# Cross-attention and quantised FFN on one core: two bias rows moved from TensorE to GpSimd, and a rewritten last half with filler matmuls on TensorE

## Chip, core and metric

The kernel runs on one NeuronCore of a Trainium2 chip. The metric is the device time of one execution in microseconds (us), lower is better. Engines are called as in the profile: PE (TensorE matmul), PEld (its weight loads), DVE (VectorE), ACT (ScalarE), POOL (GpSimd), SP (SyncE, which only issues DMAs here).

## What is computed

The reference, cut to what matters (4 batches of 1024 rows, width 256, 16 heads of 16, context of 77 rows, hidden width 1024):

```python
x = x + xattn(layernorm(x), ctx)          # Wout product + bout
x = x + ffn(layernorm(x))                 # w_proj product + b_proj

def xattn(x, mem):                        # keys: 77 context rows, then x itself
    q = x @ Wq;  k, v = split(concat(mem, x) @ Wkv)
    dots = q k^T * 16**-0.5, causal over x, all context visible
    return softmax(dots) @ v @ Wout + bout

def ffn(x):                               # both products on quantised operands
    h = block_quant(x) @ block_quant(w_fc).T + b_fc
    return block_quant(gelu(h)) @ block_quant(w_proj).T + b_proj
```

`block_quant` works on blocks of 32 along the contracted dimension: the block's largest magnitude gives a power of two, and values are rounded to 3 mantissa bits of it. The kernel does this with three steps: a reduce (largest magnitude per block), two small operations that turn it into a constant "mag", then an add of mag and a subtract of mag, which rounds.

## The kernel before, in words

Rows are handled in tiles of 128 (8 per batch, T = 32 in all). Four heads form a group, so there are 16 stages `kk` (4 batches of 4 groups). In each stage, 14 steps go over pieces of the causal score matrix; a step is two half steps. In a half step PE does the row maxima of the next stage (L563, `max_matmul`, K = 32, four of them in the four 32-row strips of the array), the scores of this stage (L627, also K = 32), and attention times values with a lag of two steps (L664, which uses all 128 rows). DVE reduces the maxima (L587, L589), ACT takes the exponentials (L638), POOL sets masked entries to zero (L643) before L664 reads them.

Everything else is cut into units, each a list of emitted stages with delays, which `run` (L1357) places into the half steps by a planner's budget: a unit has a cost in us, each of its stages a load on DVE, PE, POOL, ACT, and a stage is emitted when its delay is over and the credit of its engines is positive. Emission order is queue order: every engine runs its instructions in the order in which they are emitted. The units that the change touches:

- `bias_units` (L113) loads the three bias vectors, splits them in three bf16 parts and builds `bias3` (3 x 1536). A bias is added on PE: a matmul of `ones3` (3 x 128) with a slice of `bias3` as the last member of an accumulation group (L813 for the attention output, L965 for the FFN output, L900 for the hidden layer).
- `wout_unit` (L797): fetches a tile of x (L804, on SP's queue), multiplies attention output with Wout (L809, two f32 products) and adds the bias (L813), copies the sum out of PSUM on ACT (`evacuate`, L794), adds it to x on POOL (L817), and takes statistics. Its fetch waits until the half is `divided`, that is until the attention sums have been normalised.
- `out_unit` (L921): quantises the hidden tile, transposes it (L954), multiplies with w_proj (L962, eight products), adds the bias (L965), evacuates (L794), adds on POOL (L969) and stores.
- `last_divide` (L747) normalises a half of the last batch: sums to DRAM and back (`sm`), a reciprocal, to DRAM and back (`rows`), then two PE products that spread the rows over partitions (L768) and two DVE multiplications (L776).

The last batch has no later stage to hide behind. Its first half's output tiles run as units in stage 15, directly on DVE. The rest is `last_part` (L1099): a list of jobs, each with an engine, an estimated time, predecessors and, for PE jobs, a PSUM bank (three `s` banks, two `st` pairs). A greedy loop takes the job that can start soonest by these estimates and emits it. The jobs of a tile are `norm` (ACT), `largest` (DVE), `round` (POOL), `turn` (PE transposes, L1168), `turned` (ACT), `hidden` (PE, L896 and L900), `gelu` (ACT, L1187), `max0`, `max1` (DVE, L197 and the small L204 and L208), `add0` (DVE, L224), `add1` (POOL, L224), `sub0`, `sub1` (POOL, L229), `turn_h` (PE, L1221), `turned_h` (ACT, L1229), `project` (PE, L1236 and L1240) and `finish` (DVE, L1247, then the store L1248). The second half's tiles first need `fetch`, `invert`, `spread`, `scale`, `load` (x, L1116), `wout` (L1124, L1128), `add`, `stats` and `root`.

A start-up row of 100 matmuls of the identity (`identb`, L1417) runs on PE while the first inputs load; its results are not used.

Of the kernel before, what the change touches and what calls it, by code (L numbers as in the profile page):

```python
# [9 lines left out]
F32 = mybir.dt.float32  # L10
# [33 lines left out]
def kernel(  # L44
# [68 lines left out]
    def bias_units(dram):  # L113
# [10 lines left out]

        def split():
            for r in range(3):
                nc.vector.tensor_copy(parts[r], braw)
                if r < 2:
                    nc.vector.tensor_sub(braw, braw, parts[r])
# [8 lines left out]

    wfcT = const.tile([P, KC, HID], BF16, name="wfcT")
# [117 lines left out]
    with ExitStack() as actx:  # L257
# [489 lines left out]
        def last_divide(b, ic):  # L747
# [17 lines left out]
            def spread(k):  # L765
                def emit():
                    got[k] = s_tile([P, ICW])
                    nc.tensor.matmul(  # L768
                        got[k], sel[:, k, :], got["rows"], start=True, stop=True
                    )  # L770
                return emit
# [24 lines left out]

        def wout_unit(b, it):  # L797
# [4 lines left out]
            def fetch():  # L802
                x2[t] = xrp.tile([P, D], F32, name="x2")
                nc.sync.dma_start(out=x2[t], in_=xf[t * P : (t + 1) * P, :])  # L804

            def project():
                yp = s_tile([P, D])
                for k in range(KC):
                    nc.tensor.matmul(  # L809
                        yp, o_pk[b, ic][:, k, it * P % ICW : it * P % ICW + P], wo_sb[:, k, :],  # L810
                        start=(k == 0), stop=False,
                    )
                nc.tensor.matmul(yp, ones3, bias3[:, B_OUT : B_OUT + D], start=False, stop=True)  # L813
# [10 lines left out]
            if b == B - 1:  # L824
# [4 lines left out]
                return cost(1.8, [fetch, project, (1, add_and_collect)])  # L829
            return cost(  # L830
                1.8, [fetch, project, (2, add), (2, collect)],
                (0, 0, 0, 0), (0, 0.4, 0, 1.1), (0, 0, 0.7, 0), (0.6, 0, 0, 0),
# [59 lines left out]
        def hidden_matmuls(t):  # L892
            hp = ps_st.tile([P, 2, ICW], F32, name="st_ps")
            for n in range(HID // ICW):
# [26 lines left out]
        def out_unit(t):  # L921
# [28 lines left out]

            def turn():
# [7 lines left out]
            def project():  # L959
                yp = s_tile([P, D])  # L960
                for k in range(HC):
                    nc.tensor.matmul(  # L962
                        yp, got["hT"][:, k, :], wprT[:, k, :], start=(k == 0), stop=False
                    )
                nc.tensor.matmul(yp, ones3, bias3[:, B_PROJ : B_PROJ + D], start=False, stop=True)  # L965
                got["y"] = evacuate(yp)

            def add():
# [7 lines left out]
                [first, (1, largest(1)), (1, rounding(0)), (1, rounding(1)), turn, project, (2, add)],  # L976
                (0.7, 0, 0, 0), (1.05, 0, 0, 0), (0, 0, 2.1, 0), (0, 0, 2.1, 0), (0, 1, 0, 0.6),
# [121 lines left out]
        def last_part(b):  # L1099
# [4 lines left out]
            fetch, invert, parts = last_divide(b, 1)  # L1104
            jobs, banks = {}, {"s": (3, []), "st": (2, [])}
            got = {}
# [6 lines left out]
            def load(t):  # L1113
                def emit():
                    x2[t] = xrp.tile([P, D], F32, name="x2")
                    nc.sync.dma_start(out=x2[t], in_=xf[t * P : (t + 1) * P, :])  # L1116
                return emit

            def project(t):
                def emit():  # L1120
                    col = t * P % ICW
                    got["yp", t] = s_tile([P, D])
                    for k in range(KC):
# [28 lines left out]
            def largest(t):  # L1152
                def emit():
                    got["magx", t] = quant_steps(got["xh", t], D, "x")
# [9 lines left out]
            def turn(t):  # L1164
                def emit():
                    got["tp", t] = s_tile([P, KC, P], BF16)
# [12 lines left out]
            def hidden(t):  # L1179
                def emit():  # L1180
                    got["hp", t] = hidden_matmuls(t)
                return emit

            def gelu(t):
                def emit():
                    hs[t] = hp_.tile([P, HID], F32, name="h")
                    nc.scalar.activation(  # L1187
                        hs[t], got["hp", t].rearrange("p e n -> p (e n)"), AF.Gelu
                    )
# [6 lines left out]
            def largest_h(t, p):  # L1196
                def emit():
                    if p == 0:
                        got["amax", t] = small.tile([P, HID // QBLK], F32, name="amaxh")
                    quant_largest(hs[t][:, cols[p]], got["amax", t][:, blocks[p]])  # L1200
                    if p:
                        got["magh", t] = quant_mag(got["amax", t], "h")
                return emit

            def add_h(t, p, engine):
                return lambda: quant_add(engine, hs[t][:, cols[p]], got["magh", t][:, blocks[p]])
# [10 lines left out]
            def turn_h(t):  # L1217
                def emit():
                    got["tp", t] = s_tile([P, HC, P], BF16)
# [12 lines left out]
            def project_h(t):  # L1232
                def emit():
                    got["yp", t] = s_tile([P, D])
                    for k in range(HC):
# [9 lines left out]
            def finish(t):  # L1245
                def emit():
                    nc.vector.tensor_tensor(x2[t], x2[t], got["yp", t], ALU.add)  # L1247
                    nc.sync.dma_start(out=of[t * P : (t + 1) * P, :], in_=x2[t])  # L1248
                return emit


            job("fetch", "SP", 0.5, fetch, late=3.5)
            job("invert", "DVE", 0.6, invert, ["fetch"], late=4.2)
            for k, (spread, scale_sums) in enumerate(parts):
                job(("spread", k), "PE", 1.2, spread, ["invert"], "s", ("scale", k))
                job(("scale", k), "DVE", 0.8, scale_sums, [("spread", k)])
            for i in range(HN, NT):
                t = T[i]
                job(("load", i), "SP", 0.5, load(t), late=2.0)
                job(  # L1260
                    ("wout", i), "PE", 1.8, project(t), [("scale", k) for k in range(KC)], "s",
# [9 lines left out]
            for i, t in enumerate(T):  # L1271
# [3 lines left out]
                job(("largest", i), "DVE", 0.9, largest(t), [("norm", i)])  # L1275
                job(("round", i), "POOL", 1.3, rounding(t), [("largest", i)] + old("turn", XQ))
                job(("turn", i), "PE", 0.4, turn(t), [("round", i)], "s", ("turned", i))
# [3 lines left out]
                job(("hidden", i), "PE", 2.0, hidden(t), [("turned", i)], "st", ("gelu", i))  # L1281
                job(("gelu", i), "ACT", 1.05, gelu(t), [("hidden", i)] + old("sub1", HBUF))
                job(("max0", i), "DVE", 0.7, largest_h(t, 0), [("gelu", i)])
                job(("max1", i), "DVE", 1.1, largest_h(t, 1), [("max0", i)])
# [240 lines left out]
```

## Time and profile before

| What | Value |
|---|---|
| runs shown | 1002.62, 1004.85 (median), 1007.97 us |
| profiled execution, its own time | 1001.35 us |
| its span in the profile | 999.6 us (1.75 us lie around it) |
| mean granted PE clock over the span | 0.971 |
| end of the last attention product of the last stage (L664) | about 929.1 us |
| end of the last PE work before `last_part` (L813) | 931.6 us |
| last instruction of `last_part` on DVE (L1247) | 996.43 to 996.85 us |
| matmuls of `bias3` with 256 columns: L813, L965, L1128, L1240 | 28, 24, 4, 8 |

The profile lists busy time per engine; for PE a matmul's end is modelled, and matmuls overlap, so the distance between the starts of two instructions says more than their durations. "PEclk" is the share of PE's clock that was granted in a slice or a stretch. In groups and timelines a row reads: line, engine, operation, output<-inputs, shape, count, then busy time and mean ns, or start and duration. In the view of stretches a row reads: stretch, its length, busy us and instruction counts of PE, PEld, DVE, ACT, POOL, then PEclk, DMA share and GB/s.

### The profile page before, as it was taken

The page shows a single profiled execution, that of the slowest core. Times are in us where ns is not written, and L with a number is a line of the kernel's source. Part 1 is how long each engine was busy: PE and PEld are TensorE (multiplying, and loading weights), DVE is VectorE, ACT ScalarE, POOL GpSimd, SP SyncE. Part 2 cuts the span into 40 slices and gives each one's busy share as a digit, 9 for nine tenths or more (in the row PEclk, how much of TensorE's full clock was granted, in tenths as well). Part 3 has the DMA queues.
Part 4 walks back from the last instruction along what each step waited for, and adds up shares of the span by engine and source line. Part 5 has one row for each costly group of instructions (what it writes and reads, how often), then busy time and mean ns, then how long its engine had stood idle before and what let it go on. Part 6 is the DMA issues. An engine that isn't in the chain of part 4 may idle for free.

```text
span 999.6 us, 21255 instructions
## 1 busy us (share of the span) xinstructions
PE 955.7 (96%) x8132; PEld 410.8 (41%) x8132; DVE 638.3 (64%) x2091; ACT 560.4 (56%) x828; POOL 378.9 (38%) x784
## 2 busy tenths in 40 slices
PE   8989999999999999999999999999999999999797
PEld 5443434343444334344444344334443434334233
DVE  3868775766574766666666666646557576662575
ACT  3256564555466655665556665665555664767233
POOL 2022322231443345343625335234425246342356
PEclk9989999999999999999999999999999998999677
DMA  4021001301120001200131000200122000001100
GB/s 121 12 78 45 13 27 31 93 13 42 57 70 1 15 15 43 71 8 28 40 79 35 11 17 9 64 7 23 29 69 61 8 12 13 19 8 43 41 11 32
DMA packets 35212, 35.33 MB, mean 35 GB/s; under 512 B 13587, under 2 KB 29267, under 8 KB 35110
## 3 DMA queue, kind: packets, MB, share of 16 engines
q1 hardware_dynamic: 35086, 33.96, 12.1%
q8 instruction: 64, 1.05, 0.4%
q14 instruction: 38, 0.31, 0.1%
q10 hardware_dynamic: 24, 0.01, 0.0%
HBM read 15.60 MB, written 5.25 MB: 21 GB/s over the span
## 4 chain that ended last, share of the span: by engine, by line
PE 81%; DVE 9%; ACT 4%; POOL 2%; issue 2%; DMA 1%; SPq 0%; POOLq 0%; ACTq 0%; DVEq 0%
PE s_ps L563 34%; PE av_ps L664 16%; PE s_ps L486 6%; PE st_ps L627 5%; PE st_ps L896 4%; DVE jk L589 3%; PE s_ps L457 3%; PE s_ps L809 3%; PE s_ps L962 2%; PE st_ps L900 2%; ACT pt L638 2%; DVE mx L587 2%; PE s_ps L954 1%; PE s_ps L1124 1%; DVE amaxh L197 1%
## 5 line engine op out<-in xcount | busy, mean ns | idle before, releaser
L638 ACT ACTIVATE pt<-st_ps 128x1024 f32<-128x1024 f32 (+4 forms) x448 | 353.8, 794 | 257.6 <-PE st_ps L627 229.5
L563 PE MATMUL s_ps<-kT,qT 32*128 32x512 f32 (+2 forms) x1736 | 472.0, 530 | 14.9 <-DVE mxp L589 7.7
L627 PE MATMUL st_ps<-qT,kT 32*128 32x512 f32 (+5 forms) x1792 | 467.3, 528 | 2.5 <-ACT pt L638 2.5
L643 POOL TENSOR_SCALAR_AFFINE_SELECT pt<-pt 128x254 f32<-128x254 f32 (+3 forms) x320 | 117.8, 371 | 422.9 <-ACT pt L638 422.1
L563 PEld LDWEIGHTS s_ps<-kT,qT 32*128 32x128 f32 x1736 | 187.6, 184 | 180.7 <-issue 59.0
L589 DVE CUSTOM_DVE_ANT_0 jk<-s_ps,tri,mx 128x77 bf16<-128x77 f32 (+3 forms) x372 | 173.6, 505 | 80.5 <-PE st_ps L627 61.2
L664 PE MATMUL av_ps<-pt,vaug 128*32 128x256 f32 (+7 forms) x3072 | 221.5, 362 | 2.1 <-POOL pt L643 1.2
L589 DVE CUSTOM_DVE_ANT_0 jk<-s_ps,tri 128x512 bf16<-128x512 f32 (+3 forms) x248 | 126.6, 549 | 136.6 <-PE st_ps L627 95.7
L587 DVE TENSOR_REDUCE mx<-s_ps 128x1 f32<-128x512 f32 x248 | 159.5, 685 | 83.7 <-PE st_ps L627 78.0
L627 PEld LDWEIGHTS st_ps<-qT,kT 32*128 32x128 f32 (+1 forms) x1792 | 182.0, 182 | 12.0 <-ACT pt L638 9.5
L664 PEld LDWEIGHTS av_ps<-pt,vaug 128*32 128x32 f32 (+1 forms) x3072 | 61.8, 108 | 191.9 <-issue 133.7
L229 POOL TENSOR_TENSOR hq<-h,magh 128x512 bf16<-128x512 f32 x64 | 68.0, 1069 | 8.9 <-DVE h L224 5.7
L224 POOL TENSOR_TENSOR h<-h,magh 128x512 f32<-128x512 f32 x48 | 52.1, 1085 | 47.2 <-DVE magh L208 46.9
L197 DVE TENSOR_REDUCE amaxh<-h 128x16 f32<-128x512 f32 x64 | 42.6, 675 | 7.6 <-ACT h L1187 7.6
L896 PE MATMUL st_ps<-wfcT,xqT 128*128 128x512 bf16 x128 | 42.9, 420 | 0.5 <-ACT xqT L1176 0.5
L589 DVE DVE_READ_ACCUMULATOR2_ANT mxp<- 128x1 f32 x512 | 41.9, 82 | 0.0
L457 PE MATMUL s_ps<-wv,xT 128*128 128x256 f32 (+1 forms) x144 | 39.9, 402 | 0.3 <-ACT vaug L462 0.3
L486 PE MATMUL s_ps<-xT,wk_sb 128*128 128x512 f32 (+1 forms) x96 | 36.1, 504 | 2.4 <-ACT xT L443 1.8
L224 POOL TENSOR_TENSOR xh<-xh,magx 128x256 f32<-128x256 f32 x32 | 19.7, 617 | 41.0 <-DVE magx L208 19.7
L462 ACT COPY vaug<-s_ps 128x256 f32<-128x256 f32 (+1 forms) x36 | 14.4, 400 | 33.0 <-PE s_ps L457 32.8
L809 PE MATMUL s_ps<-wo_sb,o_pk 128*128 128x256 f32 x112 | 31.6, 405 | 1.3 <-DVE mxp L589 0.9
L794 ACT COPY y<-s_ps 128x256 f32<-128x256 f32 x48 | 18.0, 375 | 25.2 <-PE s_ps L813 13.2
(126 smaller groups left out, 845.9 us busy)
## 6 DMA issues: line engine op xcount, KB each, us to landing
kT<-k_st SPq DMA_DIRECT2D x16, 275.2 KB
xn<-in_x_dram SPq DMA_DIRECT2D x16, 256.0 KB
qT<-q_st SPq DMA_DIRECT2D x16, 256.0 KB
o_pk<-o_st SPq DMA_DIRECT2D x32, 128.0 KB
x<-in_x_dram SPq DMA_DIRECT2D x32, 128.0 KB
out_dram<-x SPq DMA_DIRECT2D x32, 128.0 KB
rb<-rd SPq DMA_DIRECT2D x96, 32.0 KB
x<-in_L_ffn_w_fc_dram SPq DMA_DIRECT2D x8, 128.0 KB
```

The source lines that it names most:

```text
L224: engine.tensor_tensor(src3, src3, magb, ALU.add)
L229: nc.gpsimd.tensor_tensor(dst.rearrange("p (n k) -> p n k", k=QBLK), src3, magb, ALU.subtract)
L457: nc.tensor.matmul(vp[:nj, :], xT[b][:, k, jt * P : jt * P + nj], wv[:, k, :], start=(k == 0), stop=(k == KC - 1),)
L486: nc.tensor.matmul(pp[:, :n], w[:, k, hi * P : (hi + 1) * P], xT[b][:, k, first + lo : first + lo + n], start=(k == 0), stop=(k == KC - 1),)
L563: nc.tensor.matmul(sp[:, 0 : hi - lo], qTs[kk % NQK][rows, it * P : (it + 1) * P], kTs[kk % NQK][rows, lo:hi], start=True, stop=True,)
L587: nc.vector.tensor_reduce(into, sp[:, 0:w], axis=AX.X, op=ALU.max)
L589: nc.vector.tensor_tensor_reduce(junk.tile([P, ICW], BF16, name="jk")[:, 0:w], sp[:, 0:w], mask, 1.0, before, ALU.add, ALU.max, into)
L627: nc.tensor.matmul(st[:nj, e, : i1 - i0], kTs[kk % NQK][rows, t * P : t * P + nj], qTs[kk % NQK][rows, i0:i1], start=True, stop=True,)
L638: nc.scalar.activation(pt[:nj, :, :w], st[:nj, :, :w], AF.Exp, scale=scale)
L643: nc.gpsimd.affine_select(out=pt[:nj, :, :behind], in_=pt[:nj, :, :behind], compare_op=ALU.is_ge, fill=0.0, base=base, pattern=[[0, 2], [1 ...
L664: nc.tensor.matmul(acc[c * PAD : (c + 1) * PAD, off + lo : off + hi], vaugs[b % 2][:nj, t, v0 : v0 + PAD], pts[kk, n, c // 2][:nj, c % 2, ...
L896: nc.tensor.matmul(hp[:, n, :], xqT[t][:, k, :], wfcT[:, k, n * ICW : (n + 1) * ICW], start=(k == 0), stop=False,)
```

## The change

Two changes. In batches 0 to 2 the biases of the attention output and of the FFN output are no longer products on PE: both vectors are loaded once, broadcast to all 128 partitions (`bo_sb`, `bp_sb`, two more DMAs on ACT's queue), and POOL adds them to the x tile in place, in a stage `lift` of its own, emitted before the product. In the last batch the bias products stay.

In the last batch, the four x tiles of the first half are fetched at the start of stage 15 (`fetch_unit`) instead of after the division, and the second half's `load` jobs wait for `fetch`. `last_part` is rewritten: every PE job is preceded by `warm`, a row of 128x128 identity matmuls into the job's own bank, four plus one for each 0.06 us that PE stands idle before the job by the planner's estimate (446 in all, by the instruction order). The table for Gelu is loaded by a dummy activation ahead of the first `norm`. The largest magnitudes and the first of the two mag operations stay in PSUM (`tops`, in the bank of `av_ps`). Gelu writes its result back into the PSUM bank of `hidden`, the reduce and the adds read it there, both adds are on DVE, and the bank is free only after `add1`. The output is evacuated on ACT (`out`) and added on POOL (`finish`). Among the jobs that can start within 0.1 us the loop takes the one with the longest way to the end.

```diff
@@ bias_units
+        for to, src in ((bo_sb, bout), (bp_sb, b_proj)):
+            nc.scalar.dma_start(out=to, in_=src.partition_broadcast(P))
@@ wout_unit
-                        start=(k == 0), stop=False,
+                        start=(k == 0), stop=(k == KC - 1 and b < B - 1),
-                nc.tensor.matmul(yp, ones3, bias3[:, B_OUT : B_OUT + D], start=False, stop=True)
+                if b == B - 1:
+                    nc.tensor.matmul(yp, ones3, bias3[:, B_OUT : B_OUT + D], start=False, stop=True)
...
-                return cost(1.8, [fetch, project, (1, add_and_collect)])
+                project.ready = lambda: (b, ic) in divided and t in x2
+                return cost(1.8, [project, (1, add_and_collect)])
+            def lift():
+                nc.gpsimd.tensor_tensor(x2[t], x2[t], bo_sb, ALU.add)
-                1.8, [fetch, project, (2, add), (2, collect)],
+                1.8, [fetch, (2, lift), (1, project), (2, add), (2, collect)],
@@ out_unit
+            def lift():
+                nc.gpsimd.tensor_tensor(x2[t], x2[t], bp_sb, ALU.add)
-                nc.tensor.matmul(yp, ones3, bias3[:, B_PROJ : B_PROJ + D], start=False, stop=True)
-                [first, (1, largest(1)), (1, rounding(0)), (1, rounding(1)), turn, project, (2, add)],
+                    first, (1, largest(1)), (1, rounding(0)), (1, rounding(1)), (2, lift), (1, turn),
+                    project, (2, add),
@@ last_part
+            tops = ps_av.tile([P, NT, NX + NH], F32, name="av_ps")
+            def warm(to):
+                for _ in range(4 + int(idle[0] / 0.06)):
+                    nc.tensor.matmul(to[:, 0:P], identb, identb, start=True, stop=True)
...
             def gelu(t):
-                    hs[t] = hp_.tile([P, HID], F32, name="h")
-                    nc.scalar.activation(
-                        hs[t], got["hp", t].rearrange("p e n -> p (e n)"), AF.Gelu
-                    )
+                    hp = got["hp", t] = got["hp", t].rearrange("p e n -> p (e n)")
+                    nc.scalar.activation(hp, hp, AF.Gelu)
...
-                    nc.vector.tensor_tensor(x2[t], x2[t], got["yp", t], ALU.add)
+                    nc.gpsimd.tensor_tensor(x2[t], x2[t], got["y", t], ALU.add)
...
+            job("table", "ACT", 1.4, lambda: nc.scalar.activation(dummy, zero, AF.Gelu))
-                job(("load", i), "SP", 0.5, load(t), late=2.0)
+                job(("load", i), "SP", 0.5, lambda t=t: fetch_x(t), ["fetch"], late=2.0)
-                job(("hidden", i), "PE", 2.0, hidden(t), [("turned", i)], "st", ("gelu", i))
+                job(("hidden", i), "PE", 1.65, hidden(t), [("turned", i)], "st", ("add1", i))
-                job(("add1", i), "POOL", 1.1, add_h(t, 1, nc.gpsimd), [("max1", i)])
+                job(("add1", i), "DVE", 0.7, add_h(t, 1), [("add0", i)])
-                job(("finish", i), "DVE", 0.5, finish(t), [("project", i)])
+                job(("out", i), "ACT", 0.4, out_of_psum(t), [("project", i)] + old("finish", 4))
+                job(("finish", i), "POOL", 0.8, finish(t), [("out", i)])
...
+                start, _, name = min((c for c in could if c[0] <= soonest + NEAR), key=lambda c: c[1:2])
+                idle[0] = start - free.get(engine, 0.0)
@@ stage 15
+                extras = [fetch_unit(t) for t in T[:HN]] + extras
                 extras += wout_units(b, 0)
```

## Prediction, made before the changed kernel was run

> **What bounds the kernel now.** I read the page first, engines and slices:
>
> ```profile
> PE 955.7 (96%) x8132; PEld 410.8 (41%) x8132; DVE 638.3 (64%) x2091; ACT 560.4 (56%) x828; POOL 378.9 (38%) x784
> PE   8989999999999999999999999999999999999797
> PEclk9989999999999999999999999999999998999677
> ```
>
> PE is busy nearly everywhere and POOL 38%, so moving work from PE to POOL is the right direction. The last three digits of the clock row are the last batch's tail (each slice is 25 us): there PE was granted 0.6 to 0.7 of its clock. The two places need separate sums. The span is cut at 932 us, where PE goes idle between the last unit (last bias product 931.6) and `last_part`.
>
> **Main part: what a bias product costs.** The timeline of PE, three places:
>
> ```profile
> 498.87 1.13 PE L809 MATMUL s_ps<-wo_sb,o_pk 128*128 128x256 f32 x4
> 499.93 0.28 PE L813 MATMUL s_ps<-bias,ones 3*128 3x256 bf16 x1
> 499.93 0.45 PE L563 MATMUL s_ps<-kT,qT 32*128 32x205 f32 x2
> ...
> 449.96 0.28 PE L965 MATMUL s_ps<-bias,ones 3*128 3x256 bf16 x1
> 450.17 1.13 PE L457 MATMUL s_ps<-wv,xT 128*128 128x256 f32 x4
> ...
> 430.04 1.13 PE L457 MATMUL s_ps<-wv,xT 128*128 128x256 f32 x4
> 431.10 0.69 PE L563 MATMUL s_ps<-kT,qT 32*128 32x512 f32 x1
> ```
>
> A bias product lasts 0.28 us, and 24 L813 and 24 L965 of batches 0 to 2 go: by durations 48 x 0.28 = 13.3 us. Starts say otherwise. In the first place L563, which uses one 32-row strip, starts in the same 0.01 us as the 3-row bias: from the first of the four products to L563 it is 499.93 - 498.87 = 1.06 us. The last place has no bias and also takes 431.10 - 430.04 = 1.06. So a bias ahead of strip products costs nothing. In the second place a 128-row product follows and starts 0.21 us later; the product ahead of such a bias also shows 0.31 to the next start where 0.22 is usual, so 0.30 us in all. I went through all 48: 33 stand ahead of strip products, 15 ahead of 128-row work. Gain: 15 x 0.30 = 4.6 us.
>
> **What POOL pays.** 48 lifts of a 128x256 addition, by the row of the same operation:
>
> ```profile
> L817 POOL TENSOR_TENSOR x<-x,y 128x256 f32<-128x256 f32 x24 | 17.3, 727 | 20.3 <-ACT y L794 20.3
> ```
>
> 48 x 0.727 = 35 us, on an engine with 620 us idle. What can suffer is a mask (L643) queued behind a lift: L664 waits for it. Of 160 masked pieces all but one have 1.2 us or more from the mask's end to the use in L664, the one 0.64; PE's idle time put down to a mask is 1.2 us in the whole span. If that cover were gone, each lift would cost up to 0.73 us. The FFN lift waits for nothing; the attention lift, emitted two half steps after its x was fetched, can wait for that DMA, with masks and rounding additions behind it on POOL. I charge 0.6 us, bounded by 0 and 2. The two broadcasts (128 KB each) are on ACT's queue in the first 10 us, when the next loads are used at 14.3 us: nothing, at worst 1 us. The lift shifts a unit's later stages by a half step; the planner then orders some of the 128-row work differently, which I can't price: between -2 and +2 us, taken as 0. **Main part: -4** (-6 to -1).
>
> **The tail.** Then I read stretches (PE, PEld, DVE, ACT, POOL, then granted clock):
>
> ```profile
> 932.00:935.00 3.00, 0.00 (x0) 0.00 (x0) 2.52 (x15) 0.00 (x0) 0.00 (x0) 0.90 0.31 93
> 946.00:948.00 2.00, 2.00 (x5) 0.37 (x5) 1.97 (x4) 0.00 (x0) 1.04 (x1) 0.50 0.00 0
> 954.00:956.00 2.00, 2.00 (x5) 1.05 (x5) 1.43 (x4) 0.00 (x0) 1.28 (x3) 0.50 0.00 0
> 984.00:986.00 2.00, 2.00 (x13) 0.68 (x11) 1.82 (x6) 1.10 (x2) 0.39 (x2) 1.00 0.18 64
> ...
> 6.00:8.00 2.00, 2.00 (x39) 2.00 (x38) 1.86 (x8) 0.00 (x0) 1.11 (x6) 1.00 1.04 345
> ```
>
> PE idles at 932 to 935 and the clock falls to 0.50. By finer stretches it is half from 934.4 to 958.3, from 968.5 to 982.2 and from 995.8 on. It changes at multiples of 3.41 us: 7 and 4 such windows. At half clock a tile's hidden product took 3.00 us, at full 1.70 us:
>
> ```profile
> 939.09 1.04 PE L896 MATMUL st_ps<-wfcT,xqT 128*128 128x512 bf16 x2 [0.46 <-ACT xqT L1176]
> ...
> 962.59 0.60 PE L896 MATMUL st_ps<-wfcT,xqT 128*128 128x512 bf16 x2
> ...
> 996.43 0.42 DVE L1247 TENSOR_TENSOR x<-x,s_ps 128x256 f32<-128x256 f32 x1 [3.64 <-PE s_ps L1240]
> ```
>
> (to the next job's start: 939.09 to 942.09, 962.59 to 964.29). A half-clock window thus costs 3.41 x (1 - 1.70/3.00), about 1.5 us of PE-bound time.
>
> The change fills PE with 446 identity products. The start-up row prices them: 39 in two full-clock microseconds, 0.056 us each in steady row; it ran from half to full clock (0.107, then 0.056) after about 4 us of nothing else, so these products count as activity. The order of instructions after puts 98 of them ahead of the first `turn`, 102 ahead of the four `turn` of the second half, 40 ahead of the last but one `turn_h`, and 4 or 5 ahead of a job with no gap.
>
> PE, with all at full clock, from the end of the last unit at 932.0 (four first-half products now stand ahead of the last L664, and the first waits 0.8 us for DVE's scale of 921.5 to 922.2; L664's end moves by 2.9 us, PE's by 0.4): hidden 8 x 1.70 = 13.6; spread 2 x 0.92 = 1.8; wout 4 x 1.27 = 5.1; `turn` 8 x 0.15 = 1.2; `turn_h` 8 x 0.45 = 3.6; project 8 x 1.19 = 9.5: 34.8 us of work. Identity products 446 x 0.056 = 25.0. With 0.5 us of waits PE ends at 932.0 + 60.3 = 992.3. PSUM drain 0.2, `out` on ACT 0.40, one hand-over 0.07, `finish` on POOL 0.76: 993.8. The last store's issue and landing took 999.6 - 996.85 = 2.75: 996.5, or 3.1 less than before. The same walk over the old job list ends 0.45 us too early, so I take **-2.7** (bounds: without any identity products the job order ends 4 us earlier; all at half clock it ends 46 us later).
>
> What hides the rest. Adds on DVE instead of POOL give DVE 8 x (0.69) more, but POOL's 1.06 us adds go and reading PSUM spares DVE an SBUF input. The row of the small mag operation shows what is at stake:
>
> ```profile
> L204 DVE TENSOR_SCALAR magh<-amaxh x32: 180/181/1034, 335.3 to 988.7; 128x32 int32<-128x32 int32 x32
> ```
>
> The same 0.18 us operation took up to 1.03 us, in the tail, beside POOL's additions. That agrees with the Trainium skill, "SBUF — State Buffer", section "Who interferes with whom": DVE and GpSimd share a port pair that one locks, and a DVE instruction with at most one SBUF input outside the two-port modes stays clear of it. By it the stall on the eight tiles would go from DVE altogether; the sum does not use that.
>
> Added waits: a `hidden` bank is held until `add1` instead of `gelu` (two pairs; the next `hidden` and its row of fillers queue behind it on PE, which is in the walk); `load` sits on SP behind `rows`, read by `add` only 10 us later: covered. The early x fetches and the Gelu table load (1.28 us, while ACT waits for `root`) cost nothing; undone, the table returns 1.28 us to the first `gelu`.
>
> **Sum.** On the profile's time: 1001.35 - 4.0 - 2.7 = 994.6. The median of the runs is 3.5 us above that execution: 998.1. I take 1 us more off because part of the spread of the runs is likely half-clock windows, whose number the change lowers: **997.0 us**. A measurement of this kernel tells about 0.5% (5 us) from no change.
>
> **Rivals.**
> (1) *The bias saving does not arrive*: PE's 4.6 us turn into waits because DVE's maxima or ACT's exponentials end last. For it: DVE 64% and waits for L589 in PE's rows (7.7 us); against: 15 places are ends of 128-row groups, where PE alone runs. Only the tail gains: 1004.85 - 2.7 = 1002. Chance 0.22, same.
> (2) *The clock falls in spite of the fillers and stays low.* In the tail of before it stayed at 0.50 through seven windows in which every stretch shows PE busy 2.00 of 2 us (the rows of 946 and 954). Once low, PE also pays 0.107 per filler. The fillers then are pure load. Price 1.54 us a window; before had 11 but not PE-bound throughout, after would be. With 11 windows 997 + 17 = 1014, slower; it decides from about 8 windows (27 us of half clock) on. For it: those rows, and drops in the main part at 835 with PE busy; against: each tail drop followed a window with PE at 0.19, 0.64 or 0.48, and the fillers remove such windows. Chance 0.14.
> (3) *A drop heals in one or two windows*: two windows, 997 + 3 = 1000, same. The start-up row is for it, the seven windows against. Chance 0.05. The Trainium skill, "TensorE: Matmul & The Clock Gate", section "What's actually happening", says this: half clock after an idle window of about 3.4 us, full after one busy one. The trace agrees at the start and disagrees at 934 to 958.
> (4) *Data come later than the planner's estimates*, or the fillers wait in front of ready work: each us of misjudged idle is one of PE; at 4 us 1001, same. Chance 0.05.
> (5) *More than forecast*, with the reordering and DVE's stalls helping: 990. Chance 0.06, faster.
> Forecast: 0.48; of its spread a little lies above the 0.5% line at 999.8 (0.02 of it). That the fillers don't act as activity, so the change doesn't do what it says, is rival 2 by another road.
>
> Faster 0.46 + 0.06, rounded up by the part of (4) that stays small: 0.53; same 0.02 + 0.22 + 0.05 + 0.04: 0.33; slower 0.14. The range must hold 8 in 10: from (5)'s 990 less 1 to 1008, past rival 1's 1002 with 3 us of the runs' spread and 3 us of unpriced order; it leaves out rival 2 and part of (5).
>
> **What would show it.** Right: PEclk at 1.00 from 935 to 990, hidden 1.70 us apart throughout, identity products at 0.056; 15 slots of 0.30 us gone ahead of 128-row work and no change at the other 33; PE's idle for masks still about 1 us; last PE work at about 988 (992.3 less the 4 of the main part). Wrong: a half-clock stretch longer than 8 us in the tail; L664 waiting on L643 by more than 2 us; PE idle time put down to DVE in the main part; `out` or `finish` waiting long after their `project`.

## Result, and the profile after

The changed kernel takes 992.18 us (median of 6 runs, 991.47 to 999.66) against 1002.76 us of the kernel before (6 runs, 1000.12 to 1007.97): ratio 0.9897, 95% interval 0.9875 to 0.9919. The profiled execution took 991.54 us, its span 989.8 us; the run of 999.66 us had a mean granted clock of 0.985 where the profiled one had 0.993. The forecast was 997.0 us, inside a range of 989 to 1008.

The page after, engines and slices, in the form of those of before:

```profile
PE 957.0 (97%) x8519; PEld 429.4 (43%) x8530; DVE 632.6 (64%) x2083; ACT 562.4 (57%) x837; POOL 405.7 (41%) x832
PE   8989999999999999999999999999999999999998
PEclk9989999999999999999999999999999999989999
```

The granted clock of the last three slices is 9 where it was 6, 7, 7. PE is as busy as before (957 against 956 us) in a span 10 us shorter. In the tail its time is no longer filled by half-clock products but by identity products at full clock.

The same stretches of the tail (length, busy PE, PEld, DVE, ACT, POOL, then granted clock):

```profile
932.00:935.00 3.00, 3.00 (x36) 2.01 (x36) 1.10 (x4) 1.54 (x3) 2.29 (x4) 1.00 0.03 5
946.00:948.00 2.00, 2.00 (x21) 1.50 (x20) 1.90 (x5) 0.00 (x0) 0.28 (x1) 1.00 0.00 0
954.00:956.00 2.00, 2.00 (x39) 2.00 (x37) 1.53 (x6) 0.77 (x3) 1.80 (x3) 1.00 0.19 66
984.00:986.00 2.00, 1.92 (x17) 1.12 (x15) 0.00 (x0) 0.62 (x2) 0.72 (x1) 1.00 0.19 66
```

The hole at 932 is filled and the clock is 1.00 in every one of them. The timeline of PE after, four places (start, duration, line; L988 is the FFN output product, L463 the value product, L1161 a filler, that is one of the identity products of `warm`, L1217 a transpose, L919 a hidden product), and below them the last addition on POOL:

```profile
448.83 1.05 PE L988 MATMUL s_ps<-wprT,hT 128*128 128x256 bf16 x8
449.71 1.03 PE L463 MATMUL s_ps<-wv,xT 128*128 128x256 f32 x4
...
925.27 5.64 PE L1161 MATMUL s_ps<-identb 128*128 128x128 bf16 x98
930.75 0.28 PE L1217 MATMUL s_ps<-identb,xq 128*128 128x128 bf16 x2
...
963.21 0.59 PE L919 MATMUL st_ps<-wfcT,xqT 128*128 128x512 bf16 x2
...
964.91 0.40 PE L1161 MATMUL s_ps<-identb 128*128 128x128 bf16 x4
```

```profile
986.46 0.72 POOL L1302 TENSOR_TENSOR x<-x,y 128x256 f32<-128x256 f32 x1 [0.69 <-ACT y L802]
```

In the first two rows the value product follows the output product with no bias slot between them: eight products in 0.88 us, 0.11 each. The 98 fillers take 5.48 us to the next start, 0.056 us each. A hidden product takes 964.91 - 963.21 = 1.70 us, its full-clock time. POOL's last addition ends at 987.18, 9.7 us before DVE's of before.

Cut at the end of the last unit on PE: 931.62 us before, 925.34 after, so the **main part gave 6.3 us**; from there to the end of the span 68.01 us before, 64.47 after, so the **tail gave 3.5 us**. (The last unit's work on PE is an output product in the old order and an attention product in the new one; the same work lies ahead of the cut in both.) Clock windows differ too: ahead of the tail the trace of before shows five windows of 3.41 us at half clock, that of after four; in the tail 11 and none, without the half clock that the end of the span cuts off.

### The profile page after: what moved, and what is told of

It is laid out like the page before. It is cut to its first block, busy times and chain, and to the rows that moved or that the text cites. A ratio compares the mean times of both kernels' runs of the same rounds, so it can differ in the third digit from the quotient of the medians.

```text
span 989.8 us, 22093 instructions
## 1 busy us (share of the span) xinstructions
PE 957.0 (97%) x8519; PEld 429.4 (43%) x8530; DVE 632.6 (64%) x2083; ACT 562.4 (57%) x837; POOL 405.7 (41%) x832
## 4 chain that ended last, share of the span: by engine, by line
PE 80%; DVE 10%; ACT 3%; issue 3%; POOL 2%; DMA 1%; SPq 0%; POOLq 0%; DVEq 0%; ACTq 0%
PE s_ps L569 36%; PE av_ps L670 16%; PE s_ps L492 6%; PE st_ps L633 4%; DVE jk L595 4%; PE st_ps L919 3%; PE s_ps L463 3%; PE s_ps L825 3%; PE s_ps L988 2%; DVE mx L593 2%; PE st_ps L923 2%; ACT pt L644 2%; PE s_ps L1161 1%; PE s_ps L980 1%; POOL hq L235 1%
## 5 line engine op out<-in xcount | busy, mean ns | idle before, releaser
L230 POOL TENSOR_TENSOR h<-h,magh 128x512 f32<-128x512 f32 x40 | 41.9, 1047 | 26.8 <-DVE magh L214 26.7
L463 PE MATMUL s_ps<-wv,xT 128*128 128x256 f32 (+1 forms) x144 | 39.5, 399 | 0.3 <-ACT vaug L468 0.3
L919 PE MATMUL st_ps<-wfcT,xqT 128*128 128x512 bf16 x117 | 36.2, 383 | 0.4
L802 ACT COPY y<-s_ps 128x256 f32<-128x256 f32 x56 | 20.9, 373 | 21.4 <-PE s_ps L988 8.5
L203 DVE TENSOR_REDUCE amaxh<-h 128x16 f32<-128x512 f32 x48 | 32.3, 675 | 0.0
L492 PE MATMUL s_ps<-xT,wq_sb 128*128 128x512 f32 x64 | 31.4, 615 | 0.0
```

The lines of the kernel that those rows point to most:

```text
L463: nc.tensor.matmul(vp[:nj, :], xT[b][:, k, jt * P : jt * P + nj], wv[:, k, :], start=(k == 0), stop=(k == KC - 1),)
L492: nc.tensor.matmul(pp[:, :n], w[:, k, hi * P : (hi + 1) * P], xT[b][:, k, first + lo : first + lo + n], start=(k == 0), stop=(k == KC - 1),)
L919: nc.tensor.matmul(hp[:, n, :], xqT[t][:, k, :], wfcT[:, k, n * ICW : (n + 1) * ICW], start=(k == 0), stop=False,)
```

## Experiments

My theory: the bias rows cost PE only where 128-row work follows; the fillers hold the clock in the tail; the rewritten jobs are a small part. Rivals: durations count in full, the clock is not what the tail lost, or the gain sits in the rewritten jobs. All medians below are beside the kernel before on the same chip. The last four columns are from each kernel's one trace: the end of the last unit on PE, the tail from there, and the half-clock windows ahead of the tail and in it (a drop that the end of the span cuts off is left out: 3.8 us in before and e8, 5.1 in e1, at most 1.6 in the others).

| Kernel | Median us | Ratio to before, 95% | Fillers | Units end | Tail | Half main | Half tail |
|---|---|---|---|---|---|---|---|
| before | 1002.8 to 1003.5 | 1 | 0 | 931.62 | 68.01 | 5 | 11 |
| changed | 992.18 | 0.9897 (0.9875 to 0.9919) | 446 | 925.34 | 64.47 | 4 | 0 |
| e1 bias rows only | 996.36 | 0.9927 (0.9912 to 0.9941) | 0 | 925.46 | 69.40 | 4 | 12 |
| e2 tail only | 1002.20 | 0.9982 (0.9969 to 0.9994) | 446 | 934.71 | 66.66 | 6 | 1 |
| e3 no fillers | 999.88 | 0.9970 (0.9957 to 0.9983) | 0 | 925.15 | 72.93 | 3 | 15 |
| e4 fillers alone | 996.26 | 0.9929 (0.9911 to 0.9947) | 316 | 929.99 | 62.76 | 3 | 2 |
| e5 bias rows and fillers | 988.21 | 0.9857 (0.9836 to 0.9878) | 316 | 925.01 | 61.39 | 4 | 1 |
| e6 fillers in idle time only | 992.14 | 0.9896 (0.9875 to 0.9917) | 294 | 929.87 | 64.28 | 6 | 3 |
| e7 four fillers a job | 999.29 | 0.9971 (0.9957 to 0.9986) | 152 | 925.45 | 71.79 | 4 | 9 |
| e8 e1 without additions | 996.19 | 0.9945 (0.9924 to 0.9966) | 0 | 928.44 | 65.87 | 6 | 9 |
| e9 Gelu into SBUF | 991.91 | 0.9882 (0.9862 to 0.9902) | 382 | 928.25 | 62.41 | 5 | 0 |
| e10 last addition on DVE | 1000.64 | 0.9976 (0.9959 to 0.9993) | 477 | 926.28 | 74.84 | 4 | 4 |
| e11 both | 999.76 | 0.9970 (0.9955 to 0.9984) | 493 | 924.91 | 71.05 | 4 | 1 |
| e12 e5, mags in PSUM | 987.38 | 0.9840 (0.9819 to 0.9861) | 316 | 926.54 | 61.23 | 5 | 2 |

### The two changes apart

e1 puts the additions of both biases into the kernel before and leaves its last part alone:

```diff
@@ wout_unit, out_unit of the kernel before (batches 0 to 2)
-                nc.tensor.matmul(yp, ones3, bias3[:, B_PROJ : B_PROJ + D], start=False, stop=True)
+            def lift():
+                nc.gpsimd.tensor_tensor(x2[t], x2[t], bp_sb, ALU.add)
```

> The kernel before with only the two bias rows of batches 0 to 2 moved to POOL; the last batch and its tail as before. My theory (15 products ahead of 128-row work cost 0.30 us each, 33 cost nothing, the lifts are covered): 4 to 5 us less than before, ratio 0.995 to 0.996, the clock of the tail as before (half for about 11 windows). Rival A (durations count, 48 x 0.28): 13 us less, ratio 0.987. Rival B (PE is not what bounds there, the gain came with the tail): within 1 us of before.

Measured 996.36 us, 6.9 less by the medians (5.9 to 8.8 by the interval). Rival A (13 us) and rival B (nothing) fall, and my 4 to 5 us were too few. In the one trace the units end 6.2 us earlier than before, with one half-clock window less, and the tail is 1.4 us longer.

What the rows themselves cost can be read by starts in the traces of before and of the changed kernel. The eight products of an FFN output stand ahead of a 128-row product in the first row, of before (the prediction shows what follows, at 449.96 and 450.17), and ahead of a 32-row strip product in the next two, of before, and the last two, of the changed kernel:

```profile
448.98 1.05 PE L962 MATMUL s_ps<-wprT,hT 128*128 128x256 bf16 x8
...
475.02 1.05 PE L962 MATMUL s_ps<-wprT,hT 128*128 128x256 bf16 x8
476.00 0.54 PE L627 MATMUL st_ps<-qT,kT 32*128 32x333 f32 x1
...
474.05 1.05 PE L988 MATMUL s_ps<-wprT,hT 128*128 128x256 bf16 x8
475.03 0.54 PE L569 MATMUL s_ps<-kT,qT 32*128 32x333 f32 x1
```

Ahead of the 128-row product it took 450.17 - 448.98 = 1.19 us with the bias row and takes 449.71 - 448.83 = 0.88 without, 0.30 less; ahead of the strip product 0.98 us in both. Over all 48 places the medians say the same: 0.30 us saved at each of the 15, 0.01 at 32 of the 33 others and 0.12 at the last. That adds up to 5.0 us. The end of the units agrees where two kernels with the same job list have the same number of half-clock windows: 926.54 and 931.62 (five: e12, before), 929.87 and 934.71 (six: e6, e2), 5.1 and 4.8 us apart. By this the rest of the 6.2 us is the window.

e2 is the reverse: the changed kernel with the bias products back on PE.

```diff
@@ wout_unit, out_unit of the changed kernel (and the two lifts and broadcasts out)
+                nc.tensor.matmul(yp, ones3, bias3[:, B_PROJ : B_PROJ + D], start=False, stop=True)
```

> The changed kernel with the biases of batches 0 to 2 back on PE and no lifts; the last half as changed. My theory: from the end of the last unit to the end of the program 64.5 us where before has 68.0, so 3 to 4 us less than before, ratio about 0.9965, and no half clock in the tail. Rival (the tail is most of the gain because the clock returns): 7 us less or more, ratio 0.993 or lower.

Measured 1002.20 us, 1.1 less by the medians and a ratio of 0.9982: less than both theories. In the trace its tail is 66.66 us, 1.4 less than before, with one half-clock window; and six windows fell ahead of the tail, one more than before and two more than in the changed kernel. With e1's 6.9 us that is 8.0 of the changed kernel's 10.6; the windows may be the rest. The gain of the whole last-batch rewrite by itself is small. e3, e4 and e5 show that it is a sum of two larger terms of opposite sign.

### Fillers and jobs apart

e3 takes the fillers out of the changed kernel, e4 puts them into the kernel before:

```diff
@@ e3: warm in last_part of the changed kernel
-                for _ in range(4 + int(idle[0] / 0.06)):
+                for _ in range(0):
@@ e4: last_part of the kernel before, ahead of each PE job
+            def warm(to):
+                for _ in range(4 + int(idle[0] / 0.06)):
+                    nc.tensor.matmul(to[:, 0:P], identb, identb, start=True, stop=True)
```

> The changed kernel without any of the 446 identity products in the last half; everything else stays. Theory 1 (the fillers are what holds the clock): half clock comes back for 7 windows or more; a hidden product then takes 3.0 us instead of 1.7, and the program ends 3 to 15 us later than the changed kernel. Theory 2 (the rewritten job order is dense enough, the fillers are load): the clock stays full in most windows and the program ends about 4 us earlier than the changed kernel, by the walk of the job order at full clock.

> The kernel before with 317 identity products ahead of the PE jobs of its own last part (four, and one for each 0.06 us of idle by its own estimates); job order and everything else as before. Theory 1 (the clock is what the old tail lost): full clock from 935 to 990, 317 x 0.056 = 18 us of fillers in PE's idle time, and an end about 4 us earlier than before, ratio 0.996. Theory 2 (the rewritten jobs bring the gain, not the clock): no faster than before, or slower by what the fillers put ahead of ready work, up to 18 us.

Without fillers 999.88 us, 7.7 more than the changed kernel; with fillers alone 996.26, 7 less than before. In both, theory 1 holds, but for two half-clock windows in e4's tail (316 fillers in its trace); and e4 gains more than the 4 us that it gave. In its trace the tail is 5.3 us shorter and the units end 1.6 us earlier, with two windows less ahead of them, which no filler touches. The clock rows of the two pages, e3 and then e4:

```profile
PEclk9989999999999999999999999999999999999576
```

```profile
PEclk9989999999999999999999999999999999999989
```

The last three digits are the whole difference. A stretch of e1 and one of e3, both with no fillers, show that this is not idleness at that moment:

```profile
946.00:948.00 2.00, 2.00 (x5) 1.04 (x5) 1.56 (x7) 0.00 (x0) 1.05 (x1) 0.50 0.00 0
```

```profile
944.00:946.00 2.00, 2.00 (x6) 0.96 (x5) 1.01 (x3) 0.89 (x1) 0.84 (x1) 0.50 0.00 0
```

PE reads busy throughout, with five or six products in 2 us, at half clock, as in the row of before at 946. With fillers in the planned idle time a drop in the tail healed after one to three windows (e2, e5 and e11 one, e4 and e12 two, e6 three; e10 has one of three and one of one; e7, with none in idle time, had three, two and four); without them it took longer: in before the last five windows of the first drop (941.2 to 958.3) had PE busy all through, in e1 four (935.2 to 948.9), and the nine of e3 from 958.9 have some idle PE time between. The Trainium skill, "TensorE: Matmul & The Clock Gate", section "What's actually happening", has full clock return after one busy window of 3.4 us. The kernels with fillers come near that; those without don't, with four and five busy windows in a row at half clock. What the gate counts as activity is not shown by these rows: the number of products and their type are not separated, and the number alone does not decide (a window of e3 with 19 products, 969.1 to 972.6, kept half clock; the last half-clock window of before's first drop had 7).

Nor do fillers prevent every drop. In e2, e4, e5, e6, e7, e10 and e12 a drop in the tail follows a window in which PE was busy throughout. In each of these windows the `spread` products, which use 16 rows, took 1.3 to 2.2 us; in the changed kernel, e9 and e11 they fall into two windows, 1.1 us in each, and the clock holds. These products alone (PE and PEld, then clock), in e5's window ahead of its drop and in the first of the changed kernel's two:

```profile
935.29:938.70 3.41, 1.82 (x4) 0.29 (x2) 1.00 0.00 0
```

```profile
934.79:938.20 3.41, 1.08 (x2) 0.29 (x2) 1.00 0.60 163
```

This is a pattern of ten traces, not a cause shown: no run moved these products, and windows ahead of the tail with 1.4 (before, 917.3) and 2.2 us of them (e8, 915.3) kept full clock. If it holds, it is partly luck, by where the windows lay, that the changed kernel's tail has no drop.

e7 keeps only the four fillers that stand ahead of every job, e6 only those for planned idle time:

```diff
@@ e7
-                for _ in range(4 + int(idle[0] / 0.06)):
+                for _ in range(4):
@@ e6
+                for _ in range(int(idle[0] / 0.06)):
```

> The changed kernel with just the four identity products ahead of each PE job, none for planned idle time (152 of 446). Theory 1 (an idle window lowers the clock, at the start above all, where 98 fillers are gone): half clock from about 928 on for at least 4 windows, slower than the changed kernel by 3 to 10 us. Theory 2 (density within the jobs is what counts): full clock after 935 and 1 to 2 us less than the changed kernel.

> The changed kernel without the four identity products that stand ahead of every PE job; those for planned idle time stay (294 of 446). Theory 1 (fillers ahead of a ready job are pure load, the clock is held by those in the idle time): 3 to 4 us less than the changed kernel, about 988.5, clock still full. Theory 2 (the four are needed): half clock returns for several windows, as slow as the changed kernel or slower.

e7 (999.29 us) is like no fillers at all: nine half windows, the first three from 928.1, 2.7 us after the units' end. So the four ahead of every job do not hold the clock without those in idle time. e6 (992.14) loses the 152 others and gains nothing: neither theory is right alone. Those 152 are 8.5 us of PE at full clock, but without them three half-clock windows came back in the tail of its trace, which is of a run of 995.88 us, 3.7 above the median.

e5 then joins the edits of e1 and e4, without any of the rewritten jobs:

> The kernel before with the bias rows of batches 0 to 2 on POOL and the identity products ahead of the PE jobs of its old last part; none of the rewritten jobs (Gelu into PSUM, adds on DVE, output through ACT and POOL, early fetch, order by the longest way). Theory 1 (the two gains are separate, each 7 us, and the rewriting gives nothing): about 989 us, ratio 0.986, 2 to 3 us faster than the changed kernel. Theory 2 (the rewriting carries part of the gain): as the changed kernel or slower, 992 us or more.

988.21 us: theory 1 holds. The gains add up, 6.9 + 7.0 of 1003.3 is 989.4, and the old jobs with fillers have a tail of 61.39 us where the rewritten ones have 64.47. Without fillers it is the same: 69.40 (e1) against 72.93 (e3); and with the bias rows on PE too: 62.76 (e4) against 66.66 (e2). **The rewritten jobs cost 3 to 4 us** of tail in all three pairs, by the medians 4.0, 3.5 and 5.9 us. The fillers shorten the tail by 8.0 us (e1 to e5), 8.5 (e3 to the changed kernel) or 5.3 (before to e4). By its interval e5 barely touches the changed kernel's (0.9878 against 0.9875); the intervals of the two other pairs lie apart.

### What POOL's additions cost

e8 is e1 with the additions left out, so batches 0 to 2 go without both biases:

```diff
-                nc.gpsimd.tensor_tensor(x2[t], x2[t], bo_sb, ALU.add)
+                pass
```

> The kernel with the bias rows moved, with the old last part, but the additions on POOL left out too: batches 0 to 2 leave out both biases. It gives the price of the 48 additions on POOL. Theory (covered but for 0 to 2 us): same as with the additions, 0 to 1 us faster, about 995.5 to 996.4. Rival (masks and roundings behind the additions cost 0.1 to 0.7 us each): 5 us faster or more, 991 or less.

996.19 against 996.36 us, with intervals that overlap: the 48 additions cost nothing that can be measured, and the rival's 5 us are excluded. In the changed kernel they are these groups (busy us, mean ns, idle before), and this is PE's whole wait for masks (total, times, longest):

```profile
L975 POOL TENSOR_TENSOR x<-x,bp_sb 128x256 f32<-128x256 f32 x24 | 18.0, 751 | 0.0
L849 POOL TENSOR_TENSOR x<-x,bo_sb 128x256 f32<-128x256 f32 x24 | 17.3, 728 | 2.5 <-DMA x<-in_x_dram 2.5
```

```profile
PE av_ps L670 <- POOL pt L649: 1.8, 4, 0.5
```

They take 35.3 us of POOL's time; 2.5 us more it waits for x at the head of the queue, and PE waits 1.8 us for masks where it waited 1.2.

### Where the rewriting loses

e9 lets Gelu write to SBUF again, so that a hidden pair is free after it; e10 has the last addition on DVE from PSUM, as before; e11 has both.

```diff
@@ e9
-                    nc.scalar.activation(hp, hp, AF.Gelu)
+                    hs[t] = hp_.tile([P, HID], F32, name="h")
+                    nc.scalar.activation(hs[t], got["hp", t].rearrange("p e n -> p (e n)"), AF.Gelu)
...
-                job(("hidden", i), "PE", 1.65, hidden(t), [("turned", i)], "st", ("add1", i))
+                job(("hidden", i), "PE", 1.65, hidden(t), [("turned", i)], "st", ("gelu", i))
@@ e10
-                job(("out", i), "ACT", 0.4, out_of_psum(t), [("project", i)] + old("finish", 4))
-                job(("finish", i), "POOL", 0.8, finish(t), [("out", i)])
+                job(("finish", i), "DVE", 0.5, finish(t), [("project", i)])
```

> The changed kernel with one part of the rewritten jobs undone: Gelu writes to SBUF again, so the PSUM pair of a hidden product is free after Gelu and not after the second addition; both additions stay on DVE (382 identity products by its own plan). Theory 1 (holding the pair is what the rewriting costs: the hidden products of the second half waited at 960.7 for the additions of an earlier tile, and those of the last two tiles came out side by side): 2 to 4 us less than the changed kernel, 988 to 990. Theory 2 (the way out through ACT and POOL costs it): as the changed kernel, 991.5 to 993.

> The changed kernel with another part undone: the last addition is DVE's again, straight from PSUM, without the copy on ACT and the addition on POOL (477 identity products by its own plan). By the rows of the last tile, ACT 0.37 + POOL 0.72 + hand-over against DVE 0.42 is 0.8 us at the end, and the two additions of 1.4 us that POOL does between the last roundings go. Theory 2: 2 us or more less than the changed kernel. Theory 1: 0.5 to 1 us less.

> Both undone: Gelu into SBUF and the last addition on DVE from PSUM; largest magnitudes in PSUM, additions on DVE, early fetch, the order by the longest way and the fillers stay (493 identity products). If these two parts are the whole 4 us that the rewriting costs, 988 or less, as the kernel with the old jobs and the fillers. If it stays above 990, the order of the jobs or the number of fillers is the rest of it.

e9: the median is the changed kernel's (991.91), as theory 2 had it. Its one trace has a tail 2.1 us shorter, 62.41, and units that end 2.9 us later beside one more half-clock window; the runs can't tell whether that tail is a gain. e10 and e11: 1000.64 and 999.76 us, 8 more, where both theories had less. Both theories fall there. PE's timeline in e10 and in e11:

```profile
965.90 6.03 PE L1161 MATMUL st_ps<-identb 128*128 128x128 bf16 x76 [3.75 <-DVE h L1255]
```

```profile
981.18 3.13 PE L1161 MATMUL s_ps<-identb 128*128 128x128 bf16 x36 [2.62 <-DVE x L1302]
```

PE waits up to 3.75 us for DVE, for the addition that frees a hidden pair (L1255) and for the last addition (L1302), which frees the bank of a product, and then still runs 76 and 36 fillers whose idle time is already over. Among jobs that can start at once the rewritten loop takes the one with the longest way to the end. On DVE that puts the last additions, which have no way left, behind the other work, and they hold banks. That is how I read the two rows; a rewritten loop with the old choice was not run. So the way out through ACT and POOL is needed with this loop, while in the old loop DVE does it with no such wait (e5).

PE in e5 and in the changed kernel, over the same 61 us:

```profile
925.00:986.00 61.00, 55.26 (x541) 35.94 (x540) 45.15 (x114) 23.89 (x33) 36.52 (x40) 0.97 0.09 29
```

```profile
925.00:986.00 61.00, 60.07 (x671) 42.69 (x674) 38.33 (x103) 27.01 (x42) 30.86 (x39) 1.00 0.09 27
```

DVE is 7 us less busy after the rewriting, and PE 5 us more, at 60.07 of 61: 130 more fillers are 130 x 0.056 = 7.3 us. What the rewriting took off DVE, its planner gave PE to do as fillers. But the fillers alone can't be the cause, since e3, with none, is 3.5 us slower than e1, with none either. PE's waits for POOL's rounding ahead of `turn` from 936 us on, in e3 and in e1 (total, times, longest):

```profile
PE s_ps L1217 <- POOL xq L235: 4.9, 4, 2.3
```

```profile
PE s_ps L1183 <- POOL xq L234: 1.2, 1, 1.2
```

In e3 the four `turn` products of the second half stand one behind another, each waiting for POOL, and three half-clock windows more fall into its tail than into e1's. The changed kernel has 102 fillers at the same place (953.76 to 959.80). So an order of jobs that leaves PE nothing else to do there is another candidate for the 3 to 4 us. The cause stays open: no run has the rewritten jobs in the old order, and the way out is not told apart either.

One rewritten part has a clear local effect, the small mag operations in PSUM. e12 adds it to e5:

```diff
-                    quant_largest(hs[t][:, cols[p]], got["amax", t][:, blocks[p]])
-                        got["magh", t] = quant_mag(got["amax", t], "h")
+                    quant_largest(hs[t][:, cols[p]], top[:, blocks[p]])
+                        got["magh", t] = mag_of(top, "h")
```

> The kernel with the bias rows on POOL, the old job list and the fillers (988.2 us), with one part of the rewritten jobs added: the largest magnitudes and the first of the two small mag operations of the last part in PSUM. In that kernel's tail the two small operations took 0.42 and 0.52 us on average for a hidden tile and up to 0.98, in the changed kernel 0.19, 12.0 against 5.8 us for all of them. Theory (DVE's chain ends last there, and the stalls beside POOL are on it): 2 to 5 us less, 983 to 986. Rival (roundings on POOL or the fillers on PE end last): 987.5 to 989.5.

The two small operations on DVE in the tail of e5, and of e12:

```profile
L213 DVE TENSOR_SCALAR magh<-magh 128x32 f32<-128x32 f32 x8 | 4.2, 523 | 0.3
L209 DVE TENSOR_SCALAR magh<-amaxh 128x32 int32<-128x32 int32 x8 | 3.3, 416 | 0.6
```

```profile
L1131 DVE TENSOR_SCALAR av_ps<-av_ps 128x8 int32<-128x8 int32 (+1 forms) x16 | 3.0, 187 | 0.5
L1135 DVE TENSOR_SCALAR magh<-av_ps 128x32 f32<-128x32 f32 x8 | 1.5, 191 | 0.6
```

Mean 0.52 and 0.42 us became 0.19. The Trainium skill, "SBUF — State Buffer", section "Who interferes with whom", says that DVE with no more than one SBUF input outside the two-port modes stays clear of GpSimd. The rows with the operands in PSUM agree; whether the slower pair of e5, which has one SBUF input too, ran in a two-port mode is shown by no run. The time did not follow: 987.38 against 988.21 us, intervals of 0.9819 to 0.9861 and 0.9836 to 0.9878, the tail 61.23 against 61.39. The rival holds (it gave 987.5 or more): the small operations were not what ended last. What did, these runs don't separate. e5 and e12 are the fastest kernels here, 4 to 5 us below the changed one.

## Why the prediction was right, and where it was off

The sign, the range and the two mechanisms (starts count and not durations, fillers hold the clock) were right, but the rewritten jobs by themselves had the wrong sign in the working; the size was three quarters of what came (7.9 us forecast from the shown median, 10.6 measured against the six runs).

- **Main part, -4 forecast, -6.3 in the profile.** The reading that starts count and durations don't held: rival A's 13 us (48 x 0.28 is 13.4) is excluded by e1, and the 15 slots of 0.30 us are found gone, 4.6 us. The other 0.4 of the 5.0 us measured by starts are the 33 slots that I priced at nothing. The term that was mis-sized is the charge for POOL: 0.6 us taken, 0.2 us between the medians of e8 and e1, which is nothing. The remaining 1.3 us go with a half-clock window less, in one trace each; the sum did not hold it at all.
- **Tail, -2.7 forecast, -3.5 in the profile.** The walk of the job order gave 996.5 - 932.0 = 64.5 us, measured 64.47. Its prices held: 1.70 for a hidden product, 0.056 for a filler, clock full throughout; PE ends 60.6 us after the cut where the walk had 60.3, and what follows took 3.9 us for 4.2. That the two errors cancel to 0.03 us is luck, and the full clock may be in part. What I subtracted for the walk's 0.45 us error in the old list was not needed.
- **What the sum hid.** I compared the new tail with the old as a whole. The walk without fillers "4 us earlier" was at full clock, which is not to be had without them: e3 ended 7.7 us later, not 4 earlier. And I did not price the old job list with fillers. e5 shows 61.39 us there, so the rewriting itself was a loss that the forecast took for part of the gain. The total came out near because the walk went by the new job list as a whole, in which the loss is already contained.
- **Base.** I set the median 3.5 us above the profiled execution and took 1 us off for clock windows. The 1004.85 us that this rests on is the median of three runs; that of the six runs of before is 1002.76, 1.4 above the profiled one. After the change the median lies 0.6 above it. Of the 4.8 us between 997.0 and 992.2, 2.3 are the main part, 0.8 the tail, and 1.8 this offset.
- **Rival 1** (no bias saving) is excluded by e1. **Rival 2** (half clock in spite of the fillers) did not come in the changed kernel's trace; its premise, half clock at full busy share, stands in e1 and e3 again. What I held against it, that each drop of the tail follows a window with PE partly idle, does not hold with fillers: the drops of e2, e4, e5, e6, e7 and e12 include one behind a window that was busy throughout. **Rival 3** (a drop heals in one or two windows) is what mostly happens in the tail with fillers, and ahead of the tail, where there are no fillers, in every trace. **Rival 4** (fillers ahead of ready work) is not excluded: e6 is no faster with 152 fillers less, but e5's PE is 5 us less busy. e10 and e11 show it plainly for other job lists.

## What to carry to other kernels

Price an instruction on PE by the distance between starts with and without it, and sort its occurrences by what follows: a bias product ahead of 32-row products was free, one ahead of 128-row products cost 0.3 us. Where the granted clock falls in a tail, try fillers alone on the old code first: here 316 identity products, for PE's planned idle time and four ahead of each job, brought 7 us, and the rewriting that came with them in the changed kernel took 3 to 4 back. Fillers count as PE time once work is ready behind them, so their number has to be set anew after any change of the job list.

## What was not expected of the hardware

In the tail, half clock lasted through up to five windows of 3.41 us in a row with PE busy all through them without fillers, and one to three with fillers in idle time; and drops began behind windows in which PE was busy throughout (above). The drops ahead of the tail came in every trace, three to six windows in all: one at 54 to 57 us and one at 883 to 896 us in each, the others at 12 to 13, 126, 438, 666, 670 to 671 or 835 us, in some traces and not in others. They move the end of the main part by several us from one trace to the next (925.15 with three windows in e3, 929.87 with six in e6, whose main part is the same). What sets their number is open.
